# A GRU over 128 steps on one core: r and z as one joint product of seven block products, in one instruction stream

## The chip, the cores and the metric

The kernel runs on one core of a Trainium2 chip. The metric is the device time of one execution in microseconds (us). TensorE (PE in the profile) multiplies matrices and writes to PSUM, VectorE (DVE), ScalarE (ACT) and GpSimd (POOL) work on rows of up to 128 partitions, SyncE (SP) issues DMAs. Each engine takes its instructions in the order in which the program lists them; the order between engines is kept by semaphores.

## The reference

A gated recurrent unit (GRU) with batch 64, 128 steps, 512 inputs and 512 hidden units, all in float32, and a residual sum at the end. Every fourth step but the last the state is passed through one more layer before the next step.

```python
def step(h, inp):
    x_t, prop = inp
    comb = jnp.concatenate([x_t, h], axis=-1)
    z = jax.nn.sigmoid(comb @ Wz + bz)
    r = jax.nn.sigmoid(comb @ Wr + br)
    comb2 = jnp.concatenate([x_t, r * h], axis=-1)
    h_cand = jnp.tanh(comb2 @ Wh + bh)
    h_new = (1.0 - z) * h + z * h_cand
    h_next = jnp.where(prop, jnp.tanh(h_new @ Wp + bp), h_new)
    return (h_next, h_new)
...
do_prop = ((t + 1) % 4 == 0) & (t < T - 1)
out = x + ys
```

## The kernel before

**Layout.** The 64 rows of the batch are two halves of 32 (`h` = 0, 1). TensorE's array is used as four strips of 32 columns: a product of one half is 32 rows high and lies on one strip, and four such products run side by side, each on its own quarter of the partitions. Each float32 product appears as two matmul records (and two weight loads) in the profile.

**Recurrent part.** A gate of one half is `gate(i, h, lT, w)`: four blocks of the hidden size (`K` = 4) times two column groups, 8 products of 256 columns on the half's two strips; the other two strips are left to the other half. A step has three gates for each half, R, Z and the candidate H, and every fourth step P. The products add onto PSUM tiles `rec_0`, `rec_1` and `rec_z` that ScalarE has filled before with the input part of that step (`seed`, from the SBUF tiles `cp`). ScalarE's sigmoid or tanh (`crossed`), VectorE's multiply and transpose (`turn`) lead to the next product of that half.

**Input part.** x times the three input weights doesn't depend on the state. It is worked out for groups of four steps by two nested levels of a seven-product scheme (Strassen's, in Winograd's form): `batch` makes two outer products as 14 units, and a unit has 4 products of 192 columns on all four strips. The units of a batch go to three PSUM banks (scratch tiles) in turn; after certain units ScalarE copies a bank or VectorE adds banks (the `end_` functions) into SBUF tiles `mb`. GpSimd adds these up to `cp` (`outer_...`, `with_bias`) and makes the sums of x that the scheme needs (`sum_...`), and adds the new state to x for the output.

**Order.** `half(h)` is a generator that yields after every product with its cost in columns. A loop at the end runs `half(0)` and `half(1)` side by side and always takes the one that is behind, 700 columns apart, so that the products of the two halves alternate on TensorE, and one half's sigmoid, multiply and transpose pass while the other half's products run. `fill(n, h)` puts n units of the input part in between, by the table `PLACES`, one row for each of eight steps. The last two steps run in `wide_step`, with products of 128 columns.

```python
def half(h):
    for t in range(T):
        ...
        yield from gate(R, h, hT, wh[R])
        ...
        yield from gate(Z, h, hT, wh[Z])
        ...
        yield from fill(places[0], h)
        yield from gate(H_, h, rhT, wh[H_])
        ...
while any(live):
    h = 0 if live[0] and (not live[1] or at[0] <= at[1]) else 1
    cost = next(halves[h], None)
    ...
        at[h] += cost
```

Of the kernel before, what the change touches and what calls it, by code (L numbers as in the profile page):

```python
# [18 lines left out]
def kernel(  # L19
# [14 lines left out]
    nc = tc.nc  # L34
# [6 lines left out]
    J = H // NQ  # L41
    C = 2
    K = D // P
    Q4 = 4
    CHUNK = 4
    FIRST = 2
    LAST = T // Q4 - 1
# [3 lines left out]

    const = ctx.enter_context(tc.tile_pool(name="const", bufs=1))
    xrp = ctx.enter_context(tc.tile_pool(name="xr", bufs=2))
    one = ctx.enter_context(tc.tile_pool(name="one", bufs=1))
    xtp = ctx.enter_context(tc.tile_pool(name="xt", bufs=2))  # L60
    mbp = ctx.enter_context(tc.tile_pool(name="mb", bufs=3))
    two = ctx.enter_context(tc.tile_pool(name="two", bufs=2))
    ps_c = ctx.enter_context(tc.tile_pool(name="ps_c", bufs=1, space=PSUM))
    ctx.enter_context(tc.manual_schedule())

    zeros = one.tile([P, 4 * J], BF16, tag="cq", name="zeros")
# [13 lines left out]
    wh = [const.tile([P, K, H], F32, name=f"wh_{i}") for i in range(3)]  # L80
    wp = const.tile([P, K, H], F32, name="wp")

    tw_all = const.tile([P, 3, S * NQ * 3 * J // 2], F32, name="tw")
# [3 lines left out]
    d5 = const.tile([P, S, NQ, 3, J // 2], F32, name="d5")  # L87
    din = const.tile([P, 3, NQ, 3, J // 4], F32, name="din")
    tt = const.tile([P, 7, 3, NQ, 3, J // 4], F32, name="tt")
    gates_in = (Wr, Wz, Wh)  # L90

    bias_in = tw_all.rearrange("p a b -> p (a b)")[:NQ, : 3 * J].rearrange("q (i j) -> q i j", i=3)
    rest = tw_all.rearrange("p a b -> p (a b)")[:NQ, 3 * J : 6 * J].rearrange("q (i j) -> q i j", i=3)
    middle = const.tile([NQ, 3, J], BF16, name="middle")

    def part(q):
        return slice(q * V, (q + 1) * V)

# [15 lines left out]

    xr = {}

    def new_xr(g):
        xr[g] = xrp.tile([P, Q4, S, J], F32, tag="xr", name=f"xr_{g}")
# [13 lines left out]
    h_rows = tw_all[:, 2, : S * J].rearrange("p (h u) -> p h u", h=S)  # L132
    h_init = two.tile([P, S, J], F32, tag="h", name="h_init")
    bias_x = const.tile([P, C, S, 3, J // 2], F32, name="bias_x")
    bias_p = const.tile([P, S, J], F32, name="bias_p")
# [8 lines left out]
    for i, b in enumerate((br, bh, bz)):  # L144
# [16 lines left out]
    def load_wh(i):  # L161
        load_w(wh[i], gates_in[i][D:])

    xs = {}

    def load_xs(g):
        if g * Q4 < T:
            xs[g] = one.tile([P, Q4, S, J], F32, tag=f"xs{g % 2}", name=f"xs_{g}")
            load_x(xs[g], g * Q4, Q4)

    def later_loads():
        new_xr(1)
        load_x(xr[1], Q4, Q4)
        load_xs(2)
        load_x(xr[0], 0, 2)
        load_w(wp, Wp)
        for q in range(NQ):
            nc.sync.dma_start(
                out=bias_p[part(q)],
                in_=bp.rearrange("(o d c j) -> c o d j", o=1, d=2, c=2)[q % 2].broadcast_to(  # L180
                    [V, S, J]
                ),
            )


    P_ = 3
    rec = [ps_c.tile([P, 2, 2, J], F32, name=f"rec_{n}") for n in ("0", "1", "z")]
    z = rec[2][:, 1]

    def gate_ps(i, h):  # L190
        return rec[2][:, 0] if i == Z else rec[h][:, 0 if i == R else 1]

    scratch = [ps_c.tile([P, 4 * J], F32, name=f"scratch_{n}") for n in "qraxy"]
    q_ps, r_ps, a_ps, *x_two = (
        s[:, : 3 * J].rearrange("p (m h v) -> p m h v", m=2, h=S) for s in scratch
    )
    q_bank, r_bank, a_bank, *x_banks = range(5)
    r_ = scratch[r_bank][:, 3 * J :]

    def quarters(v):  # L200
        return v.rearrange("p n (d c j) -> p c n d j", d=2, c=2)
# [10 lines left out]
    def spread(bank, rows, which):  # L212
        bank = bank.rearrange("p (i d j) -> p i d j", i=len(which), d=2)
        for d in range(2):
            for h in range(S):
                for c in range(2):
                    nc.tensor.matmul(
                        bank[part(2 * h + c), :, d],
                        lhsT=picks[:, 2 * d + c],
                        rhs=thirds[:, rows],  # L220
# [4 lines left out]
        for j, i in enumerate(which):  # L225
            nc.scalar.copy(
                bias_x[:, :, :, i, :].rearrange("p n d u -> p d n u"),
                bank[:, j].rearrange("p d (n u) -> p d n u", n=C),
            )

    bias0 = bias_x[:, 0]
    bias_d = const.tile([P, S, 3, J // 2], F32, name="bias_d")

    def idle(n):
        for i in range(n):
            nc.tensor.matmul(
                rec[i // NQ % 3].rearrange("p a d n -> p (a d n)")[part(i % NQ)],
# [6 lines left out]
    def products(ps, h, left, rhs, start=False):  # L244
        for c in range(2):
            nc.tensor.matmul(  # L246
                ps[part(2 * h + c)],
                lhsT=left,
                rhs=rhs(c),
                start=start,  # L250
                stop=True,
                skip_group_check=True,
            )
# [6 lines left out]
    def product(ps, h, lT, w, k, start=False):  # L260
# [15 lines left out]
    def crossed(dst, h, i, func, ordered=True):  # L276
        for d in range(2):
            o, v = dst[ts(d, 2 * V)], gate_ps(i, h)[ts(h, 2 * V), d, :]
            if ordered:
                o, v = state_order(o), plain_order(v)  # L280
# [937 lines left out]
```

## Time and profile before

| | |
|---|---|
| time, median of 3 runs | 1255.37 us (1254.85 to 1255.91) |
| profiled execution: span from first to last instruction | 1253.6 us |
| busy PE, DVE, ACT, POOL | 1246.9, 806.2, 830.0, 908.8 us |
| granted TensorE clock | full in all 40 slices |

The span of the profiled execution is 1.8 us under the median; what lies around the span is taken as these 1.8 us. In the profile's groups, a row has line, engine, operation, what is written and read, the shape, the count, then busy time in us and the mean of one in ns, then idle time before them. The timeline has start and duration in us. "Busy" of PE is a union over its four strips.

### The profile page before, as it was taken

Reading aid. Unit: us, or ns where it says so; the run is one execution under the profiler, and the core shown is the slowest. Engines: PE = TensorE matmul, PEld = TensorE weight load, DVE = VectorE, ACT = ScalarE, POOL = GpSimd, SP = SyncE. Lnnn points to the kernel's source line nnn. Section 1 sums busy time; section 2 is a strip of 40 time slices with the busy share of each in tenths; the row PEclk is TensorE's granted clock in tenths of the full one; section 3 lists DMA queues with packets and bytes.
Section 4 is the critical chain, followed back from the end, with each engine's and each line's share of the span. In section 5 each row is a group of like instructions: output and inputs, shape, how many; then the busy total and the mean of one; then the engine's idle time right before and its main releaser. Section 6 shows DMA issues by size and latency. Waiting matters only on the chain.

```text
span 1253.6 us, 61573 instructions
## 1 busy us (share of the span) xinstructions
PE 1246.9 (99%) x26384; PEld 1174.0 (94%) x26384; DVE 806.2 (64%) x2177; ACT 830.0 (66%) x2666; POOL 908.8 (72%) x1032
## 2 busy tenths in 40 slices
PE   9999999999999999999999999999999999999998
PEld 5899999999999999999999999999999999999987
DVE  5666666666666666666666666666666666666554
ACT  2566666766666676766666667666666666666664
POOL 4988777777876778767778677786777777777630
PEclk9999999999999999999999999999999999999999
DMA  8311212121111110221201211111111112111011
GB/s 257 83 31 42 53 37 53 36 54 39 35 53 49 41 49 24 53 53 37 54 24 49 53 41 50 36 43 47 53 38 39 49 39 53 39 52 27 12 39 35
DMA packets 112360, 61.14 MB, mean 49 GB/s; under 512 B 12844, under 2 KB 109368, under 8 KB 112088
## 3 DMA queue, kind: packets, MB, share of 16 engines
q1 hardware_dynamic: 111656, 56.90, 16.8%
q8 instruction: 208, 3.41, 1.2%
q14 instruction: 64, 0.52, 0.1%
q0 software_dynamic: 256, 0.14, 0.1%
q10 hardware_dynamic: 176, 0.16, 0.0%
HBM read 40.38 MB, written 16.78 MB: 46 GB/s over the span
## 4 chain that ended last, share of the span: by engine, by line
PE 99%; DMA 1%; SPq 0%; DVE 0%; issue 0%; ACT 0%
PE rec L246 44%; PE rec_z L246 16%; PE scratch_r L246 14%; PE scratch_q L246 11%; PE scratch_a L246 5%; PE scratch_y L246 4%; PE scratch_x L246 4%; DMA wx<-in_L_cond_Wr_dram 1%; PE scratch_a L541 0%; PE scratch_r L541 0%; PE scratch_q L541 0%; PE scratch_y L541 0%; PE scratch_x L541 0%; SPq L127 0%; SPq L141 0%
## 5 line engine op out<-in xcount | busy, mean ns | idle before, releaser
L246 PE MATMUL rec<-wh,rhT 128*32 128x256 f32 x4032 | 370.1, 379 | 0.0
L246 PE MATMUL rec<-wh,hT 128*32 128x256 f32 x3008 | 276.2, 379 | 0.0
L246 PE MATMUL rec_z<-wh,hT 128*32 128x256 f32 x3008 | 276.2, 379 | 0.0
L246 PEld LDWEIGHTS rec<-wh,rhT 128*32 128x32 f32 x4032 | 247.5, 110 | 16.7 <-ACT rec L442 0.3
L281 ACT ACTIVATE scratch_r<-rec 64x128 f32<-64x128 f32 x504 | 126.0, 250 | 129.9 <-PE rec L246 65.4
L442 ACT COPY rec<-cp 64x256 f32<-64x256 f32 x504 | 186.9, 371 | 19.4 <-DVE cp L483 0.2
L246 PEld LDWEIGHTS rec_z<-wh,hT 128*32 128x32 f32 x3008 | 190.5, 110 | 6.2
L246 PEld LDWEIGHTS rec<-wh,hT 128*32 128x32 f32 x3008 | 184.0, 110 | 11.2 <-ACT rec_z L442 0.4
L281 ACT ACTIVATE rec_z<-rec_z 64x128 f32<-64x128 f32 x488 | 122.0, 250 | 91.3 <-PE rec_z L246 79.7
L281 ACT ACTIVATE c<-rec 64x128 f32<-64x128 f32 x504 | 136.7, 271 | 61.5 <-PE rec L246 50.4
L968 POOL TENSOR_TENSOR xr<-xr,h 128x256 f32<-128x256 f32 x125 | 109.3, 874 | 85.8 <-DVE h L1138 71.9
L711 POOL TENSOR_TENSOR cp<-mb,mb 128x768 f32<-128x768 f32 x76 | 139.1, 1830 | 9.4 <-DVE mb L677 5.7
L711 POOL TENSOR_TENSOR mb<-mb,mb 128x768 f32<-128x768 f32 x58 | 106.3, 1832 | 45.8 <-DVE mb L677 45.8
L711 POOL TENSOR_TENSOR cp<-mb 128x768 f32<-128x768 f32 x46 | 84.3, 1832 | 56.8 <-ACT rec_z L442 55.4
L246 PE MATMUL scratch_r<-tw,s 128*32 128x192 f32 x928 | 120.9, 326 | 0.0
L650 ACT COPY cq<-scratch_q 128x384 f32<-128x384 f32 x212 | 102.1, 481 | 19.4 <-PE scratch_q L246 17.9
L667 DVE TENSOR_TENSOR cx<-scratch_r,cx 128x384 f32<-128x384 f32 x106 | 59.0, 557 | 84.5 <-PE scratch_r L246 69.0
L246 PE MATMUL scratch_q<-tt,s 128*32 128x192 f32 x928 | 103.6, 326 | 0.0
L1102 DVE SCALAR_TENSOR_TENSOR keep<-rec_z,h 128x256 f32<-128x256 f32 x91 | 38.6, 424 | 95.6 <-ACT rec_z L281 89.2
L673 DVE TENSOR_TENSOR mb<-scratch_q,cx 128x384 f32<-128x384 f32 x106 | 59.0, 557 | 62.5 <-ACT cq L650 62.5
L1081 DVE TENSOR_TENSOR rh<-scratch_r,h 128x128 f32<-128x128 f32 x188 | 54.8, 292 | 59.2 <-ACT scratch_r L281 59.2
L246 PE MATMUL rec<-wp,hT 128*32 128x256 f32 x992 | 91.4, 379 | 0.0
(250 smaller groups left out, 3899.9 us busy)
## 6 DMA issues: line engine op xcount, KB each, us to landing
out_dram<-xr SPq DMA_DIRECT2D x250, 64.0 KB, 1.8
xr<-in_x_dram SPq DMA_DIRECT2D x248, 64.0 KB, 2.1
xs<-in_x_dram SPq DMA_DIRECT2D x240, 64.0 KB, 2.1
wx<-in_L_cond_Wz_dram SPq DMA_DIRECT2D x2, 512.0 KB
wx<-in_L_cond_Wh_dram SPq DMA_DIRECT2D x2, 512.0 KB, 9.5
wh<-in_L_cond_Wr_dram SPq DMA_DIRECT2D x2, 512.0 KB
wh<-in_L_cond_Wz_dram SPq DMA_DIRECT2D x2, 512.0 KB, 5.5
wh<-in_L_cond_Wh_dram SPq DMA_DIRECT2D x2, 512.0 KB
```

The costliest lines, as they stand in the source:

```text
L246: nc.tensor.matmul(ps[part(2 * h + c)], lhsT=left, rhs=rhs(c), start=start, stop=True, skip_group_check=True,)
L281: nc.scalar.activation(o, v, func)
L442: nc.scalar.copy(gate_ps(i, h)[rows].rearrange("p d (c n) -> p d c n", c=C), G[t][rows, :, :, i, :].rearrange("p c d n -> p d c n"),)
L650: nc.scalar.copy(c[:, :nm], ps[:, :nm])
L667: nc.vector.tensor_add(T2[what][:, :nm], r_ps[:, :nm], T2[what][:, :nm])
L673: nc.vector.tensor_add(blocks(1, 1), runs(q_ps[:, :nm]), runs(T2[what][:, :nm]))
L711: nc.gpsimd.tensor_add(dst, a, b)
L968: nc.gpsimd.tensor_add(o, o, h_new.rearrange("p h (k e) -> p h e k", k=K))
L1081: nc.vector.tensor_mul(rh[:, h, :], r_, h_old[:, h, :])
L1102: nc.vector.scalar_tensor_tensor(out=kept[0], in0=kept[1], scalar=1.0, in1=kept[2], op0=ALU.subtract, op1=ALU.mult,)
```

## The change

Nearly all of the step is written anew. One instruction stream takes the place of the two generators: `step(t, h_old)` lists every instruction of a step in order, and `fill(n)` inserts n units of the input part at six places of a step (eight where P is run), by a new table `PLACES` with four rows.

R and Z are made by one seven-product scheme over both halves of the batch and both halves of the hidden size: seven left factors are kept in `ht` (`S1`, `A11`, `S2`, `A12`, `S3`, `S4`, `A22`, sums of quarters of the transposed state), the right factors are blocks of the joint weights `wrz` and three sums of them, `tr`. `rz(region, slot, right)` is one of the seven, 8 products of 128 columns over all four strips. The results are put together by four VectorE adds in a step (`n1` into `gx`, three into the banks B and C, `row[0]` and `row[1]`), which also add the input part of R and Z; two of them lie between products that add onto the same bank. The roles of the halves alternate: `L` = t % 2, `E` = 1 - t % 2. The candidate and P are `full(...)`, 16 products of 128 columns over all four strips for one half.

The input part keeps its scheme, with other bank use: ScalarE now makes five copies in a batch (`end_1`, `end_5`, `end_2`, `end_3`, `end_4`), VectorE two adds (`end_6`, `end_7`). GpSimd's sums stay in `mb`, and `send` moves them by four DMAs each on SP's queue into `gx`, in the layout of the state. ScalarE copies the candidate's input part from `gx` to PSUM at the end of the step before (`seed_h`). The last steps have no form of their own; the groups 2 to 31 are all made by the scheme.

```diff
+    def four_tiles(region, left, rhs, start=False):
+        for q in range(NQ):
             nc.tensor.matmul(
-                ps[part(2 * h + c)],
+                region[part(q)],
...
-    def gate(i, h, lT, w):
-        for k in range(K):
-            products(gate_ps(i, h), h, lT[:, h, ts(k, V)], lambda c: quarters(w)[:, c, k])
-            yield S * J
...
+        def end_1():
...
+            nc.scalar.copy(a_x, u_x)
+        def end_5():
...
+            nc.scalar.copy(made["e"], e_x)
+        def end_6():
+            nc.vector.tensor_add(e_x, u_x, made["e"])
+        def end_2():
+            nc.scalar.copy(blocks(0, 0), runs(a_x))
+        def end_7():
+            nc.vector.tensor_add(blocks(1, 1), runs(u_x), runs(made["e"]))
+        def end_3():
+            nc.scalar.copy(blocks(0, 1), runs(e_x))
+        def end_4():
+            nc.scalar.copy(blocks(1, 0), runs(u_x))
+        seq = []
+        for ps, j, start, end in (
+            (u_x, 1, True, end_1),
+            (e_x, 5, True, end_5),
+            (u_x, 6, False, end_6),
+            (a_x, 2, False, end_2),
+            (u_x, 7, False, end_7),
+            (e_x, 3, False, end_3),
+            (u_x, 4, False, end_4),
+        ):
...
+    def send(q, n, g, i):
+        new_gx(q)
+        for h in range(S):
+            for d in range(2):
+                nc.sync.dma_start(
+                    out=gx[q][ts(d, 2 * V), :, h, n], in_=M[g, i][ts(h, 2 * V), :, d]
+                )
...
+    def sum_rz():
+        nc.vector.tensor_sub(tr_block(3), wrz_block(0, 1), wrz_block(1, 1))
...
+    def early(v):
+        turn(a21_ps, v[:, : 2 * V])
+        turn(ht[:, A22], v[:, 2 * V :])
+        nc.vector.tensor_add(ht[:, S1], a21_ps, ht[:, A22])
+    def early_copy():
+        nc.scalar.copy(s1_ps, ht[:, S1])
+    def late(v):
+        turn(ht[:, A11 : A12 + 1].rearrange("p n v -> p (n v)"), v)
+        nc.scalar.copy(a12_ps, ht[:, A12])
+        nc.vector.tensor_sub(
+            ht[:, S2 : S3 + 1],
+            s1_a21_ps,
...
-    PLACES = (
-        (1, 7, 6), (1, 7, 0), (6, 8, 0), (6, 8, 0), (1, 8, 5), (1, 7, 0), (6, 8, 0), (6, 6, 0),
-    )
+    PLACES = {
+        0: (2, 2, 2, 1, 1, 3, 0, 0),
+        1: (4, 2, 2, 1, 0, 3, 0, 0),
...
+        3: (4, 2, 2, 1, 0, 2, 2, 1),
+    }
...
+            fill(next(places))
+            rz(e_ps, S1, raw(0, 1), start=True)
+            n1 = G[t][:, :, 1, :2].rearrange("p h g u -> p h (g u)")
+            nc.vector.tensor_add(n1, bcast(e_ps), n1)
+            fill(next(places))
+            rz(u_ps, A11, raw(0, 0), start=True)
+            nc.vector.tensor_add(row[0][:, :J], u_ps, rz_in(t, L, 0))
+            late_2()
+            fill(next(places))
+            rz(u_ps, S2, summed(2))
+            nc.vector.tensor_add(row[0][:, J : 2 * J], u_ps, rz_in(t, L, 1))
+            rz(row[0][:, :J], A12, raw(1, 0))
+            fill(next(places))
+            rz(u_ps, S3, summed(3))
+            nc.vector.tensor_add(
+                row[1][:, : 2 * J].rearrange("p (n j) -> p n j", n=2),
...
+            rz(row[0][:, J : 2 * J], S4, raw(1, 1))
+            gates(0)
+            gates_z(0)
+            fill(next(places))
+            rz(row[1][:, :J], A22, summed(4))
+            gates(1)
+            gates_z(1)
```

Three places show the order. TensorE before, at the start of a step: R of half 0 (`rec_128`) and half 1 (`rec_129`) and then Z, with units of the input part (`scratch`) between them.

```order
L246 MATMUL rec_128<-wh_92,hT_5332 32x256 x2
L246 MATMUL scratch_q<-d_97,o_8_5049 32x192 x2
L246 MATMUL rec_128<-wh_92,hT_5332 32x256 x2
L246 MATMUL scratch_r<-tw,s_8_5052 32x192 x2
L246 MATMUL scratch_r<-d_97,s_8_5052 32x192 x2
L246 MATMUL rec_128<-wh_92,hT_5332 32x256 x2
L246 MATMUL rec_129<-wh_92,hT_5332 32x256 x2
```

TensorE now, from the second candidate of step 20 (`bank_C` from `wc`) into step 21: four units (`x_107`, `x_105`, `x_104`), S1 (`bank_E`), two units, A11 (`bank_A` from `wrz`), two units, S2 (`bank_A` from `tr_89`) and A12 (`bank_B` from `wrz`).

```order
L243 MATMUL bank_C<-wc,rhT_4889 32x128 x16
L503 MATMUL x_107<-wx,s12r_4344 32x192 x4
L503 MATMUL x_105<-tt,xT_4156 32x192 x8
L503 MATMUL x_104<-tw,o_6_4737 32x192 x4
L243 MATMUL bank_E<-wrz,ht 32x128 x8
L503 MATMUL x_104<-wx,o_6_4737 32x192 x4
L503 MATMUL x_107<-tw,s_6_4740 32x192 x4
L243 MATMUL bank_A<-wrz,ht 32x128 x8
L503 MATMUL x_107<-wx,s_6_4740 32x192 x4
L503 MATMUL x_104<-tt,s_6_4740 32x192 x4
L243 MATMUL bank_A<-tr_89,ht 32x128 x8
L243 MATMUL bank_B<-wrz,ht 32x128 x8
```

The halves no longer alternate, and S2 and A12 stand next to each other. In the built program the first matmul of A12 waits for the VectorE add that reads S2 (the one into `row[0][:, J : 2 * J]`, which lies in A12's bank), and the first matmul on `x_107` after S1 waits for ScalarE's copy out of `x_107` (`end_3`).

ScalarE before, over the second half of a step: tanh (`c`), the seeds (`cp`), then two copies of the input part, then the next step's sigmoids.

```order
L281 ACTIVATE c_7984<-rec_128 64x128 x2
L442 COPY rec_128<-cp_7541 64x256
L281 ACTIVATE c_7984<-rec_129 64x128 x2
L442 COPY rec_129<-cp_7541 64x256
L442 COPY rec_z<-cp_7541 128x256
L650 COPY cx_6_8024<-scratch_y 128x384
L650 COPY cq_6_8034<-scratch_q 128x384
L281 ACTIVATE scratch_r<-rec_128 64x128 x2
```

ScalarE now, at the same place of steps 20 and 21: both tanh (`c`), `early_copy` (L724) and `late`'s copy (L728) out of `ht`, two seeds (`gx`), and behind them the input part's `end_3` (from `x_107`), `end_4`, `end_1` and `end_5`.

```order
L902 ACTIVATE c_4890<-bank_B 128x128
L902 ACTIVATE c_4890<-bank_C 128x128
L724 COPY bank_B<-ht 128x64
L728 COPY bank_C<-ht 128x64
L745 COPY bank_B<-gx_4409 128x128
L745 COPY bank_C<-gx_4409 128x128
L532 COPY mb_1_4900<-x_107 128x2x6x32
L535 COPY mb_1_4900<-x_105 128x2x6x32
L516 COPY x_106<-x_104 128x384
L520 COPY e_6_5121<-x_107 128x384
```

The copies of the input part now stand behind four copies that belong to the state, and the second of these waits for the state's last transpose.

VectorE now, at that place: `keep`, the transpose of x (`xT`), `end_7` (L529), then the first half's multiply, subtract, two short transposes and add (`early`), the second half's multiply, subtract and transpose (`late`), and `late`'s subtract.

```order
L879 SCALAR_TENSOR_TENSOR keep_4891<-bank_A,hprop_4795 128x256
L262 STREAM_TRANSPOSE xT_5000<-xs_3885 128x2x4x32
L529 TENSOR_TENSOR mb_1_4900<-x_105,e_1_4919 128x2x6x32
L903 TENSOR_TENSOR bank_A<-c_4890,bank_A 128x128
L904 TENSOR_TENSOR h_5015<-bank_A,keep_4891 128x128
L239 STREAM_TRANSPOSE bank_B<-h_5015 128x64
L239 STREAM_TRANSPOSE ht<-h_5015 128x64
L721 TENSOR_TENSOR ht<-bank_B,ht 128x64
L903 TENSOR_TENSOR bank_A<-c_4890,bank_A 128x128
L904 TENSOR_TENSOR h_5015<-bank_A,keep_4891 128x128
L239 STREAM_TRANSPOSE ht<-h_5015 128x128
L729 TENSOR_TENSOR ht<-bank_B,ht 128x128
```

What the input part needs of VectorE (here `end_7`) stands in one list with the state's chain, and in other steps behind it.

More of the change, by code (lines that the diff above doesn't have):

```diff
@@ L130, in load_wx, with load_xs @@
         )
[L132 to L135, printed above, removed]
+    def load_xs(g):
+        if g < GROUPS:
+            xs[g] = one.tile([P, Q4, S, J], F32, tag=f"xs{g % 2}", name=f"xs_{g}")
+            load_x(xs[g], g * Q4, Q4)
     new_xr(0)
@@ L536 @@
[L536 to L553 removed]
+    gx, G = {}, {}
@@ L1182 @@
+    task("s12_2", lambda: [sum_s12(2), did.add(("s12", 2))], "pair1", 28, after=tuple(("join", 2, i) for i in range(4)))
+    task(("free73", 0), lambda: None, "pair2", 14)
+    for d in range(DUOS):
+        sums(d)
+    fill(4)
+    h = h_init
+    for t in range(T):
+        if t == 1:
+            load_xs(3)
+        h = step(t, h)
 _INS = [
```

1225 lines of the change are left out of this document (525 added, 700 removed), and 5 rows, old and new, of tables (HEAD, PLACES).

## The prediction

> **What bounds the kernel now.** I read the page first, then stretches of time, the groups by shape, one tile's rows, and the timeline of the last steps, which have products of 128 columns.
>
> ```profile
> PE 1246.9 (99%) x26384; PEld 1174.0 (94%) x26384; DVE 806.2 (64%) x2177; ACT 830.0 (66%) x2666; POOL 908.8 (72%) x1032
> ...
> PE 99%; DMA 1%; SPq 0%; DVE 0%; issue 0%; ACT 0%
> ```
> ```profile
> core 0: us, PE busy (x) PEld busy (x) DVE busy (x) ACT busy (x) POOL busy (x), PEclk, DMA share, GB/s
> 71.80:1224.10 1152.30, 1152.30 (x24282) 1099.02 (x24277) 748.72 (x2013) 787.13 (x2529) 855.39 (x968) 1.00 0.16 43
> 1224.10:1253.60 29.50, 25.42 (x758) 23.01 (x750) 14.06 (x48) 12.20 (x43) 2.61 (x3) 1.00 0.14 35
> ```
> ```profile
> L246 PE MATMUL rec<-wh,hpT x992: 376/379/403, 71.8 to 1225.0; 128*32 128x256 f32 x199
> ```
>
> TensorE is the bound: it is never idle from 71.8 us, where step 4 begins (its R is the first product with `hpT`), to the start of step 124, whose R ends with the last such record at 1225.0 and so starts near 1224.1. These 120 steps take 1152.3 us, 76.8 for eight. A gain must come from fewer columns; a loss comes from anything that makes TensorE wait.
>
> **Prices.** Rows of the timeline (start, duration):
>
> ```profile
> 602.31 0.55 DVE L676 TENSOR_TENSOR mb<-scratch_r,cq 128x384 f32<-128x384 f32 x1
> 602.78 0.55 DVE L677 TENSOR_TENSOR mb<-scratch_y,cq 128x384 f32<-128x384 f32 x1
> ```
> ```profile
> 1240.95 0.28 PE L541 MATMUL scratch_r<-wh,rhT 128*32 128x128 f32 x2
> ...
> 1241.83 0.28 PE L541 MATMUL scratch_q<-wh,hT 128*32 128x128 f32 x2
> ...
> 1242.70 0.28 PE L541 MATMUL scratch_r<-wh,rhT 128*32 128x128 f32 x2
> ```
> ```profile
> 1243.33 0.31 DVE L284 STREAM_TRANSPOSE hT<-h 128x128 f32<-128x128 f32 x1
> ...
> 1243.69 0.30 PE L541 MATMUL scratch_a<-wh,hT 128*32 128x128 f32 x2
> ```
> ```profile
> 1248.44 1.08 PE L541 MATMUL scratch_y<-wh,rhT 128*32 128x128 f32 x28
> ...
> 1249.57 0.28 ACT L1045 ACTIVATE c<-scratch_y 128x128 f32<-128x128 f32 x1 [0.59 <-PE scratch_y L541]
> 1249.88 0.29 DVE L1046 TENSOR_TENSOR z<-c,z 128x128 f32<-128x128 f32 x1
> 1250.20 0.29 DVE L1052 TENSOR_TENSOR xr<-z,xr 128x128 f32<-128x128 f32 x1
> ```
>
> A product of 16 matmuls of 128 columns (32 records) starts every 0.87 us: eight waves of four records, 0.109 each. So `full` costs 0.87, `rz` (half as many) 0.436, and a unit (8 records of 192 columns, so two waves 1.5 times as wide) 2 × 1.5 × 0.109 = 0.327; I take 0.325. As a test, eight steps of before are 26 gate products of 1.744 and 98 units: 77.2, 0.5% over the 76.8.
>
> A result travels so: the last record of a product ends at 1249.52, ScalarE starts at 1249.57; a record lasts 0.27 and starts one wave before the product's end, so a reader starts 0.27 + 0.05 - 0.11 = 0.21 after TensorE could go on. ScalarE to VectorE and VectorE to itself take 0.03. TensorE starts 0.05 after the transpose that it waits for, and its next wave comes 0.02 late. VectorE operations that don't need each other overlap by 0.08 (602.31 + 0.55 against 602.78).
>
> ```profile
> L284 DVE STREAM_TRANSPOSE rhT<-rh 128x128 f32<-128x128 f32 x256 | 79.8, 312 | 8.8
> L297 DVE STREAM_TRANSPOSE xT<-xs 128x256 f32<-128x256 f32 x120 | 74.7, 642 | 2.2 <-issue 0.4
> L1136 DVE TENSOR_TENSOR rec_z<-c,rec_z 128x128 f32<-128x128 f32 x244 | 71.8, 294 | 17.9 <-ACT c L281 14.3
> ...
> L676 DVE TENSOR_TENSOR mb<-scratch_r,cq 128x384 f32<-128x384 f32 x106 | 58.0, 547 | 0.2 <-PE scratch_r L246 0.2
> ...
> L1102 DVE SCALAR_TENSOR_TENSOR keep<-rec_z,h 128x256 f32<-128x256 f32 x91 | 38.6, 424 | 95.6 <-ACT rec_z L281 89.2 <-PE rec L246 6.3
> ...
> L354 DVE TENSOR_TENSOR d<-wx 128x768 f32<-128x768 f32 x2 | 1.8, 951 | 0.0
> ```
> ```profile
> L281 ACT ACTIVATE c<-rec 64x128 f32<-64x128 f32 x504 | 136.7, 271 | 61.5 <-PE rec L246 50.4
> L281 ACT ACTIVATE scratch_r<-rec 64x128 f32<-64x128 f32 x504 | 126.0, 250 | 129.9 <-PE rec L246 65.4 <-DVE mb L676 50.5 <-DVE rhT L284 0.6
> ...
> L650 ACT COPY cq<-scratch_q 128x384 f32<-128x384 f32 x212 | 102.1, 481 | 19.4 <-PE scratch_q L246 17.9
> L442 ACT COPY rec_z<-cp 128x256 f32<-128x256 f32 x126 | 47.5, 377 | 41.0 <-DVE h L1138 36.3 <-DVE cp L483 4.1 <-POOL cp L711 0.6
> ```
>
> Two shapes have no row. A ScalarE copy of 128 columns I take as 0.27 and one of 64 as 0.20, on the line through 0.377 (256) and 0.481 (384). A transpose of 64 lies between 0.16 and 0.31; I take 0.20, since its cost falls nearly with its columns.
>
> **The change part by part.**
>
> *Fewer columns.* R and Z of a step cost 7 × 0.436 = 3.05 for 3.49. TensorE's work for eight steps is 8 × 3.05 + 16 × 0.872 (candidate) + 4 × 0.872 (P) + 98 × 0.325 = 73.7: 3.1 less than 76.8.
>
> A page speaks against products half as wide: the Trainium skill, "TensorE: Matmul & The Clock Gate", "Back-to-back issue gap", gives about 81 ns per matmul of 128 columns when each has its own weight load. By that figure the 24,900 records of 128 columns of the new kernel alone would take about 2.0 ms (an estimate from that page). The rows above differ, 0.87 us for 32, or 27 ns, with four strips side by side; the measurement decides.
>
> *A12 behind S2.* Nothing stands between them, and A12 waits for the VectorE add that reads S2: 0.21 + 0.29 + 0.05 + 0.02 = 0.57 in each of 127 steps. Before, the other half's products lay there.
>
> *A22 behind the add of 256 columns.* 0.21 + 0.42 + 0.07 = 0.70 after S3; S4 hides 0.44. Where no unit stands there (six steps of eight) 0.26 is left. The other adds between products are covered by one or two units, and so are the chains to the candidates (sigmoid, multiply, transpose: 1.25 from A22 against 1.85) and, with four units and S1 ahead, to A11.
>
> *Units behind the end of a step.* This is the largest term. 49 units for four steps and 14 for a batch: the pattern repeats after eight steps, 4 to 11, 12 to 19 and so on. Take step 21 (5 in the first pattern). Zero is the end of step 20's second candidate. VectorE has `keep` 0.42, the transpose of x 0.64 and `end_7` 0.55 ahead of the first half's multiply, which starts at 0.07. Then: multiply and subtract 0.66, two transposes 0.36, add 0.14 before the next overlaps it, multiply and subtract 0.66, transpose 0.35: 2.24. There `late`'s subtract and ScalarE's copy start; the seeds wait for the subtract: 2.56 and 2.86; `end_3` runs from 3.16 to 3.64. The unit that writes its bank again can start at 3.73. TensorE is there after four units, S1 and one unit, at 2.17. It waits 1.56, and the whole stream with it. The same sum for the others, with what each unit waits for:
>
> step 4: `end_1` 0.18. 5: `end_3` 1.56. 6: `end_7` 1.66. 7: `end_7` 0.65, first P 0.13. 8: none. 9: `end_6` 0.91. 10: `end_6` 1.06. 11: `end_1` 1.56, first P 0.54. Sum 8.3.
>
> *Eight steps:* 73.7 + 8 × 0.57 + 6 × 0.26 + 8.3 + some 25 restarts of 0.02 and S1's 0.05 = 88.8, against 76.8. Bounds: transposes of 0.16 give 88.4; no overlap on VectorE gives 92.9; if ScalarE and VectorE reach the end of a step 0.5 us earlier, six waits shrink by 3.0 to 85.8.
>
> *The sums by DMA.* Copies to `cp` go, four DMAs for each come.
>
> ```profile
> L711 POOL TENSOR_TENSOR cp<-mb,mb 128x768 f32<-128x768 f32 x76 | 139.1, 1830 | 9.4 <-DVE mb L677 5.7
> ```
> ```profile
> L102 SPq DMA_DIRECT2D xr<-in_x_dram x256: 311/432/1773, 19.8 to 1201.5; - x128
> ```
> ```profile
> xr<-in_x_dram SPq DMA_DIRECT2D x248, 64.0 KB, 2.1
> ```
>
> The tightest is the second block of an even group, in the step ahead of its use: two adds 3.7, four issues 1.7, landing 2.1: 7.5 us, with about 9 until ScalarE needs it. Nothing, if the landing stays under 3.6. If not, ScalarE stands at the seed, and behind it the copies and the sigmoids.
>
> *Head.* Three sums and one difference of the joint weights (1024 columns, 1.23 each on the slope of the 0.951 row) and four transposes of x stand in step 0 ahead of VectorE's multiply, the differences of the input weights and four transposes in step 1. TensorE has some 5 us of cover for 17; waits as above fall in steps 1 to 3. I add 9 us (0 to 20): step 4 starts at 81.
>
> *Tail.* All units are used up by step 124. Steps without cover wait for S1 1.0, A11 0.4, S2 and A12 0.6 each, A22 0.3, the candidate 0.5, beside 4.8 of work: 8.3, the first 7.3. After the last product 4.1 as before (1249.5 to 1253.6): 36.3 for 29.5.
>
> *Sum:* 81 + 15 × 88.8 + 36.3 = 1449 as the span, and 1.8 around it: 1451 us.
>
> **The rivals.**
>
> *Copies in time.* Only A12 and A22 wait fully, and units a tenth of it (1.5). Eight steps 81.4, in all 81 + 1221 + 36 + 2 = 1340. For it: ScalarE is busy 66% now, and has idle time. Against it: its copies stand in one list behind the state's chain. Chance 0.12.
>
> *Late sums.* A landing of 4 to 6 us makes one seed in eight steps wait 1 to 3: 1466 to 1496. For it: SP issues 16 more DMAs for four steps. Against: the DMA engines are 16% busy. Chance 0.14.
>
> *Narrow products.* The weight load ends up beside the stream instead of under it.
>
> ```profile
> L246 PEld LDWEIGHTS rec<-wh,rhT 128*32 128x32 f32 x4032 | 247.5, 110 | 16.7 <-ACT rec L442 0.3 <-ACT scratch_r L281 0.2
> ```
>
> One load takes 110 ns, 6,200 on each strip: up to 0.68 ms more, 2.1 ms. This is the page's rule as a mechanism of this kernel; the 0.87 above speaks against it. Chance 0.02.
>
> *Fed all the same (faster).* If TensorE doesn't stand at A12 and at the units, because results return within what is queued, only the columns count: 76 + 15 × 73.7 + 33 + 2 = 1216. It decides where the waits of eight steps sum to less than 3.1, a quarter of my sum; A12's alone, with nothing queued between, is 4.6. Chance 0.04, with 0.01 of it near the tie.
>
> **How the numbers follow.** My forecast has 0.68, and the time is its own, 1451. The range 1370 to 1510 holds nearly all of it, with the bounds 85.8 and 92.9 (1406 to 1513), the head's bounds and the late sums; the other 0.18 are outside. Measurement can tell 0.2% from no change: faster 0.03, same 0.01, slower 0.96.
>
> **What would show it.** Right: PE idle before the product that writes bank B after S2, about 0.57 for each, released by the VectorE add into bank B; idle before units, released by the ScalarE copies and by `end_6` and `end_7`; 88 to 89 us between every second P; a last stretch of about 36. Wrong: PE idle released by DMA or GpSimd, a wave of more than 0.11, or eight steps near 81 or 74.

## The result: 1504.3 us, 1.198 times the time before

The changed kernel takes 1504.29 us (median of 4 runs, 1501.6 to 1508.97), the kernel before 1255.64 beside it: a ratio of 1.198, 95% interval 1.196 to 1.201. The forecast was 1451 with a range of 1370 to 1510, so the time lies 6 us inside its upper bound. The profiled execution took 1501.6 with a span of 1499.8.

The page of the changed kernel: busy times, the chain that ended last, and the granted clock by slice.

```profile
PE 1284.1 (86%) x37368; PEld 1096.2 (73%) x37368; DVE 892.5 (60%) x2864; ACT 566.2 (38%) x1959; POOL 924.5 (62%) x1051
...
PEclk9999999999999999999999999999999999999999
...
PE 55%; DVE 25%; issue 8%; ACT 4%; DMA 3%; POOL 2%; DVEq 1%; SPq 1%; ACTq 0%; POOLq 0%
```

TensorE, 99% busy before, is 86% busy, and the chain that was 99% TensorE now runs for a quarter through VectorE. A row of the next view has a stretch and its length, busy times in the order PE, PEld, DVE, ACT, POOL, and the granted clock third from the end. 88.7 is the start of S1 of step 4, 1460.2 that of step 124.

```profile
40.30:88.70 48.40, 42.31 (x1112) 35.18 (x1116) 27.04 (x77) 15.95 (x52) 33.66 (x38) 0.97 0.23 62
88.70:1460.20 1371.50, 1184.48 (x34792) 1016.14 (x34780) 816.79 (x2666) 532.92 (x1843) 861.75 (x982) 1.00 0.29 72
1460.20:1499.80 39.60, 24.30 (x712) 18.07 (x704) 21.27 (x75) 9.44 (x41) 7.92 (x6) 0.97 0.21 49
```

The 120 steps take 1371.5 us, 91.4 for every eight where before took 76.8. What TensorE waited for is in its table of waits (who waited and for whom, idle time in us, how often, the longest):

```profile
PE bank_B L243 <- DVE bank_B L848: 61.9, 126, 0.6
PE x L503 <- DVE mb L529: 36.2, 30, 1.8
PE x L503 <- DVE x L523: 33.2, 31, 3.6
PE x L503 <- ACT x L516: 20.8, 15, 1.4
PE x L503 <- ACT mb L532: 17.6, 15, 1.3
PE bank_C L243 <- DVE bank_C L852: 13.1, 64, 0.2
```

These are the three kinds of wait that the prediction named: A12 (first row), units (L503, four rows), A22 (last). No wait of the steps is put down to a DMA. How two waits for A12 look in the timeline (start, duration, and in brackets idle time and who ended it):

```profile
297.25 0.64 PE L243 MATMUL bank_A<-tr,ht 128*32 128x128 f32 x16
297.97 0.30 DVE L848 TENSOR_TENSOR bank_B<-bank_A,gx 128x128 f32<-128x128 f32 x1 [0.64 <-PE bank_A L243]
298.32 0.64 PE L243 MATMUL bank_B<-wrz,ht 128*32 128x128 f32 x16 [0.42 <-DVE bank_B L848]
```
```profile
307.83 0.64 PE L243 MATMUL bank_A<-tr,ht 128*32 128x128 f32 x16
308.55 0.30 DVE L848 TENSOR_TENSOR bank_B<-bank_A,gx 128x128 f32<-128x128 f32 x1 [0.64 <-PE bank_A L243]
308.96 0.41 PEld L243 LDWEIGHTS bank_B<-wrz,ht 128*32 128x32 f32 x16 [0.75 <-ACT mb L535]
308.99 0.64 PE L243 MATMUL bank_B<-wrz,ht 128*32 128x128 f32 x16 [0.51 <-DVE bank_B L848]
```

In the first, S2 starts at 297.25 and TensorE could go on 0.44 later; A12 starts at 298.32, so the wait is 1.07 - 0.44 = 0.63. The table shows 0.42 for it: it counts idle time from the end of the last record, which here lies 0.2 behind the moment at which TensorE could have gone on, so each wait costs 0.2 more than its row. In the second, the wait is 1.16 - 0.44 = 0.72.

Counted so from start to start between 88.7 and 1460.2, TensorE's waits in eight steps come to 5.6 us at A12 (0.63 to 0.81 a step, 0.70 on average), 8.3 at units, 2.3 at A22 and 0.9 at the first product of P. The table agrees: for A12 (61.9 + 126 × 0.2) / 15.9 = 5.5 over the whole run, and for the units, without the one wait of 3.6 ahead of step 4, (104.2 + 90 × 0.2) / 15 = 8.1.

The products themselves have the forecast's price: of the 4,612 waves of 128 columns in these steps the median is 0.109, and 4,401 take 0.112 or less; nearly all others are the first wave of a product, at 0.13.

### The profile page after: what moved, and what is told of

It reads as the page before. It is cut to its first block, busy times and chain, and to the rows that moved or that the text cites. A ratio compares the mean times of both kernels' runs of the same rounds, so it can differ in the third digit from the quotient of the medians.

```text
span 1499.8 us, 85372 instructions
## 1 busy us (share of the span) xinstructions
PE 1284.1 (86%) x37368; PEld 1096.2 (73%) x37368; DVE 892.5 (60%) x2864; ACT 566.2 (38%) x1959; POOL 924.5 (62%) x1051
## 4 chain that ended last, share of the span: by engine, by line
PE 55%; DVE 25%; issue 8%; ACT 4%; DMA 3%; POOL 2%; DVEq 1%; SPq 1%; ACTq 0%; POOLq 0%
PE x L503 22%; PE bank_B L243 13%; PE bank_A L243 10%; PE bank_C L243 8%; DVE h L904 3%; DVE bank_C L852 3%; DVE bank_A L903 3%; DVE bank_B L848 3%; DVE ht L239 2%; DVE mb L529 2%; DMA gx<-mb 2%; DVE x L523 2%; DVE bank_B L239 1%; PE bank_E L243 1%; DVE ht L729 1%
## 5 line engine op out<-in xcount | busy, mean ns | idle before, releaser
L561 POOL TENSOR_TENSOR mb<-mb,mb 128x768 f32<-128x768 f32 x167 | 304.1, 1825 | 152.1 <-ACT mb L535 138.2
L243 PE MATMUL bank_B<-wrz,ht 128*32 128x128 f32 x4128 | 165.0, 275 | 63.1 <-DVE bank_B L848 61.9
L243 PEld LDWEIGHTS bank_B<-wrz,ht 128*32 128x32 f32 x4128 | 111.9, 109 | 95.7 <-DVE bank_B L848 42.7
L243 PE MATMUL bank_A<-tr,ht 128*32 128x128 f32 x4064 | 162.2, 275 | 1.9 <-DVE bank_B L844 1.9
L503 PE MATMUL x<-tt,s 128*32 128x192 f32 x1920 | 120.6, 328 | 50.4 <-DVE x L523 29.6
L243 PE MATMUL bank_B<-wc,rhT 128*32 128x128 f32 x4096 | 137.2, 273 | 1.4 <-ACT bank_E L766 1.0
L243 PE MATMUL bank_C<-wc,rhT 128*32 128x128 f32 x4096 | 137.2, 273 | 0.0
L243 PEld LDWEIGHTS bank_A<-tr,ht 128*32 128x32 f32 x4064 | 115.6, 110 | 29.0 <-DVE bank_B L844 22.2
L243 PEld LDWEIGHTS bank_B<-wc,rhT 128*32 128x32 f32 x4096 | 120.2, 110 | 7.3 <-ACT bank_E L766 1.7
L243 PEld LDWEIGHTS bank_C<-wc,rhT 128*32 128x32 f32 x4096 | 116.2, 110 | 0.2
L503 PEld LDWEIGHTS x<-tt,s 128*32 128x32 f32 x1920 | 61.3, 110 | 66.8 <-ACT x L516 24.8
L523 DVE TENSOR_TENSOR x<-x,e 128x384 f32<-128x384 f32 x108 | 60.0, 556 | 62.1 <-PE x L503 47.1
```

The costliest lines, as they stand in the source:

```text
L243: nc.tensor.matmul(region[part(q)], lhsT=left, rhs=rhs(q), start=start, stop=True, skip_group_check=True,)
L503: nc.tensor.matmul(v[part(2 * h + c)], lhsT=left[:, ts(h, V)], rhs=right[:, c::2], start=start and m == 0 and n == 0, stop=True, skip_grou ...
L523: nc.vector.tensor_add(e_x, u_x, made["e"])
L561: nc.gpsimd.tensor_add(flat(M[g, i]), flat(M[g, i]), flat(M[g2, j]))
```

## The experiments

**e1: A12 ahead of the add that reads S2.**

```diff
             rz(u_ps, S2, summed(2))
-            nc.vector.tensor_add(row[0][:, J : 2 * J], u_ps, rz_in(t, L, 1))
             rz(row[0][:, :J], A12, raw(1, 0))
+            nc.vector.tensor_add(row[0][:, J : 2 * J], u_ps, rz_in(t, L, 1))
```

> Edit: A12 stands ahead of the VectorE add that reads S2, so A12 no longer waits for it; the add now waits for A12, and S3 for the add. Theory (the order in which readers and writers of a bank are listed makes TensorE wait, and the waits add up): the 126 waits of A12 (61.9 us idle in the trace of the change, 5.2 us per eight steps) go, and S3 takes over a smaller one, 0.25 + 0.30 + 0.05 behind A12 less the one unit of 0.33, about 0.28 a step or 2.2 per eight: 88 us for eight steps, 1504 - 48 = about 1455 us. Rival (the follow-ups of the units, tied to the end of a step, set the pace): what A12 no longer waits the units wait longer, no change, 1495 to 1504. Rival (chain of the state alone): A12's 0.44 leaves the chain from the first to the last product of a step, the same 1455; this run does not tell that from the theory.

Measured: 1455.28 us, ratio to before 1.159 (1.157 to 1.161); eight steps 88.2 (here and below the median of the groups of eight steps, from every second P to the next). The theory's number, to the microsecond. TensorE's waits in this run:

```profile
PE x L503 <- DVE mb L529: 36.2, 30, 1.7
PE x L503 <- ACT x L516: 19.4, 15, 1.4
PE x L503 <- ACT mb L532: 18.4, 15, 1.3
PE x L503 <- DVE x L523: 17.3, 16, 3.6
PE x L503 <- POOL o L366: 16.0, 15, 1.1
```

The row of A12 is gone, and the rows of the units are nearly what they were: they did not take over the time. S3 waits instead, mostly too shortly for the table to list it. The second row below is S3; the unit ahead of it costs 0.33, so S3 starts 0.27 late, where the theory has 0.28:

```profile
302.31 0.51 PE L503 MATMUL x<-wx,xT 128*32 128x192 f32 x8
302.91 0.65 PE L243 MATMUL bank_A<-tr,ht 128*32 128x128 f32 x16
```

From step 4 to 123, S3's waits come to 2.3 for eight steps, and at A12 only restarts of 0.02 are left. As the expectation says, this run alone does not tell the theory from a chain of the state alone. One wait of the units changed hands. Half of those for L523 are now put down to GpSimd's sum of x (L366), which ends last there.

**e2: the first units of a step ahead of the copies that end the step before.** `PLACES_0` is the first number of the next step's row.

```diff
+        fill(PLACES_0(t + 1))
         early_copy()
         late(h_new[:, E])
         seeds()
...
-            fill(next(places))
+            next(places)
             rz(e_ps, S1, raw(0, 1), start=True)
```

> Edit: the units that open a step are listed, with their ScalarE copies and VectorE adds, ahead of the copies and the subtract that end the step before; TensorE's own order is the same. Theory (units wait because their copies stand behind the state's in one list): the waits of units (8.8 us per eight steps in the trace of the change, the first P's among them) fall to 3 to 4, eight steps near 86, 1504 - 86 = about 1418 us. Rival (ScalarE and VectorE are simply late, whatever the order): the copies of 0.48 and adds of 0.55 now delay the state by as much as they gain, 1490 to 1520; if they delay it in every step by 0.5, 127 x 0.5 = 64 slower, up to 1570.

Measured: 1416.82 us, ratio 1.128 (1.126 to 1.129); eight steps 86.0. TensorE's waits:

```profile
PE bank_B L243 <- DVE bank_B L851: 65.6, 127, 0.6
PE bank_C L243 <- DVE bank_C L855: 19.3, 95, 0.2
PE x L503 <- DVE mb L529: 15.0, 15, 1.0
PE x L503 <- DVE x L523: 7.2, 16, 1.8
```

The waits for ScalarE's copies (L516, L532) are gone and those for VectorE a third: 22 us in all where 108 stood. The copies were not late because ScalarE had too much to do, but because they stood behind the state in its list.

**e3: narrow units.** A unit's products have 32 columns for 192.

```diff
-                        v[part(2 * h + c)],
+                        v[part(2 * h + c)][(slice(None), 0, 0) if g >= 4 else ...],
                         lhsT=left[:, ts(h, V)],
-                        rhs=right[:, c::2],
+                        rhs=right[:, c, 0] if g >= 4 else right[:, c::2],
```

> Edit: from the fourth group on, each product of a unit has 32 columns for 192; every copy, add, wait and DMA stays. The sums of the input part are incomplete. If TensorE's columns set the time, eight steps lose 98 x 0.27 = 26.5 us, about 1504 - 400 = 1100. Theory (waits behind results): what the units no longer cover becomes waiting. A step without any unit took 8.80 us at the end of the changed kernel's trace, and a step with P takes some 2.5 more: 6 x 8.8 + 2 x 11.3 = 75 for eight steps is the least, and the waits of units stay partly: 78 to 84, so 1300 to 1390 us.

Measured: 1503.45 us in its one run, no change at all. Neither number came. The stretches show two instances of one kind of step (steps 30 and 38, both third in a pattern of eight that begins with step 4), with the granted clock third from the end:

```profile
386.51:397.22 10.71, 9.18 (x280) 7.95 (x281) 5.24 (x18) 3.26 (x11) 3.59 (x2) 0.68 0.12 34
480.48:489.28 8.80, 6.78 (x281) 5.86 (x281) 5.27 (x18) 3.14 (x10) 3.60 (x2) 1.00 0.14 37
```

The same 280 records take 10.71 us at a clock of 0.68 and 8.80 at 1.00. In a slow stretch a product of 16 records starts 0.84 after the one before, where 0.44 is the rule:

```profile
709.36 1.09 PE L243 MATMUL bank_A<-tr,ht 128*32 128x128 f32 x16
710.20 1.11 PE L243 MATMUL bank_B<-wrz,ht 128*32 128x128 f32 x16
```

So the columns that were taken out came back as waits and as a slower clock: groups of eight steps took 88.5 us at a mean clock of 0.94 and 94 at 0.82. At the full clock the theory's floor stands: the shortest instance of each of the eight kinds of step, all at a clock of 0.99 or 1.00, was 9.35, 12.09, 8.80, 11.68, 8.90, 9.94, 10.16 and 12.48, together 83.4, against 91.4, though TensorE had 26.5 less to do.

**e4: the same edit on the kernel before.**

> The same edit on the kernel before: the units' products have 32 columns for 192 from the fourth group on, all else stays; the sums of the input part are incomplete. If columns alone bound it, eight steps fall from 76.8 by 26.5 to 50, about 1255 - 410 = 850 us; GpSimd alone is busy for 909 and so the floor is above that. Theory: two streams hide each other's chains; the chain of one half sets a floor lower than the 76.8, and lower than that of the changed kernel: 1000 to 1190 us. Rival (the kernel before stands at its chain's floor as well, and the columns were only just as long): 1240 to 1255.

Measured: 1171.04 us, one run. The stretch of the 120 steps, and TensorE's largest wait:

```profile
70.00:1134.00 1064.00, 961.80 (x24199) 780.02 (x24194) 741.49 (x2013) 782.81 (x2526) 853.72 (x967) 1.00 0.18 46
```
```profile
PE rec L246 <- DVE hT L284: 78.8, 97, 1.2
```

Eight steps took 70.6 (the median; the first group, whose units are in part still wide, 78), where columns alone would be 50. So the kernel before has a floor as well, and its largest wait is for the transposes of its own state, but the floor lies below its 76.8 of columns. The changed kernel's 83.4 at full clock lies above its 73.7. The change lowered the columns by 3 and raised by 13 what the kernel, in this order of its instructions, doesn't go under. Whether two streams or plain products give the lower floor, these two runs do not tell.

**e5: the edits of e1 and e2 together.**

> Edit: the edits of the first two runs together (A12 ahead of the add; the first units of a step, with their copies and adds, ahead of the copies that end the step before). Theory (separate waits that add up): the two gains add, 49 + 87 = 136, 1504 - 136 = about 1368 us, and eight steps near 82.5. Rival (one chain is behind both, so that what one edit frees the other waits for): less than the sum, 1390 to 1417 us.

Measured: 1367.65 us, ratio 1.088 (1.086 to 1.090). The two gains, 49 and 87.5, add to within a microsecond, so the rival, one chain behind both, is out.

**e6: one stream with plain products of r and z.** Each half's gate is `full`, 16 products, as in `first_step`; ScalarE seeds r, z and the candidate in one copy. The table `PLACES` is another one, the roles of the halves no longer alternate, and the sums of weights in the first step go.

```diff
-            rz(e_ps, S1, raw(0, 1), start=True)
-            ...
-            rz(row[1][:, :J], A22, summed(4))
+            plain_product(0, R)
+            gates(0)
+            fill(next(places))
+            plain_product(1, R)
+            gates(1)
+            fill(next(places))
+            plain_product(0, Z)
+            gates_z(0)
+            fill(next(places))
+            plain_product(1, Z)
+            gates_z(1)
...
-            early(h_new[:, L])
+            turn(hT[:, ts(L, J)], h_new[:, L])
```

> Edit: the joint seven-product scheme for r and z undone alone; one instruction stream, the sums by DMA and the input part stay. r and z are 8 block products in full width for each half, seeded by ScalarE; a unit or two between them. TensorE's columns are those of the kernel before, about 77 us for eight steps. Theory (the seven products are made one after another from sums and put together by adds, and each such add is a wait): the stream of plain products has next to no waits, since R of one half covers the other half's transpose and Z covers R's sigmoid, multiply and transpose: 78 to 79.5 for eight steps, 1275 to 1315 us in all. Rival (one stream in place of two is what fails to hide the chains): eight steps near 88 or more, 1450 us or more.

Measured: 1306.96 us, ratio 1.041 (1.039 to 1.043); eight steps 79.6.

```profile
PE 1274.6 (98%) x39400; PEld 1148.7 (88%) x39400; DVE 644.1 (49%) x1844; ACT 592.7 (45%) x1705; POOL 925.2 (71%) x1051
```

With 8 × 0.436 = 3.5 us more columns for eight steps this form is 197 us faster than the change, and TensorE is 98% busy: one stream as such does not fail to hide the chains. The 4% that are left to the kernel before hold the one stream, the sums by DMA (ScalarE's seeds wait for them 17 times here, 19.2 us) and a table that was not searched for; these were not told apart. The joint product, in one stream and in this order, costs the rest.

**e7: one wait less in the state's chain.**

```diff
-                out=keep, in0=z_ps, scalar=1.0, in1=h_old, op0=ALU.subtract, op1=ALU.mult
+                out=h_new, in0=z_ps, scalar=1.0, in1=h_old, op0=ALU.subtract, op1=ALU.mult
...
-            nc.vector.tensor_sub(h_new[:, h], z_h, keep[:, h])
+            nc.vector.tensor_sub(h_new[:, h], z_h, h_new[:, h])
```

> Edit: VectorE writes keep into the tile of the new state, so that keep, off the chain, waits for GpSimd to be done with that tile, and the first half's subtract waits for its multiply alone. Theory (a second wait in front of an operation costs time even where it was met long ago: in the trace of the change the first half's subtract, with two waits, starts 0.11 us after its multiply, and the second half's, with one, 0.04): the gap falls to 0.04, the state comes 0.06 us earlier in 127 steps, where the chain is waited for: 1496 to 1500 us, and in any case the rows of the trace show 0.04. Rival (the 0.11 belongs to the first half's operands or to what runs beside it): the gap stays 0.11 and the time 1502 to 1509.

Measured: 1492.99 us (1490.03 to 1496.47), ratio 1.189 (1.186 to 1.191), against 1.198 (1.196 to 1.201). VectorE's timeline of the changed kernel, multiply and subtract of both halves in one step:

```profile
600.54 0.30 DVE L903 TENSOR_TENSOR bank_A<-c,bank_A 128x128 f32<-128x128 f32 x1 [0.33 <-ACT c L902]
600.95 0.29 DVE L904 TENSOR_TENSOR h<-bank_A,keep 128x128 f32<-128x128 f32 x1
...
601.89 0.28 DVE L903 TENSOR_TENSOR bank_A<-c,bank_A 128x128 f32<-128x128 f32 x1
602.21 0.29 DVE L904 TENSOR_TENSOR h<-bank_A,keep 128x128 f32<-128x128 f32 x1
```

And of e7:

```profile
597.91 0.29 DVE L905 TENSOR_TENSOR bank_A<-c,bank_A 128x128 f32<-128x128 f32 x1
598.24 0.29 DVE L906 TENSOR_TENSOR h<-bank_A,h 128x128 f32<-128x128 f32 x1
```

The first half's subtract started 0.11 after its multiply (600.95 - 600.84) and now starts 0.04 after it (598.24 - 598.20); the median over 127 steps falls from 104 to 34 ns. The row of line 904 in the changed kernel shows what stood between:

```profile
L904 DVEq EVENT_SEMAPHORE  x125: 21/21/21, 70.6 to 1485.8; - x125
```

An instruction of its own on VectorE's queue carries one of the two waits; e7 has none for its line 906. 0.07 a step is 9 us; the spans of the two profiled executions differ by 8.6, the medians by 11, and the intervals don't meet. The time lies 3 us under the theory's range. The operands are not the cause: the second half's subtract has the same ones in the changed kernel and started 0.04 after its multiply.

**e8: all edits, and units put where the rows show waits.** `PLACES` has eight rows, and its first number is the units ahead of the end of the step before:

```diff
-        0: (2, 2, 2, 1, 1, 3, 0, 0),
-        1: (4, 2, 2, 1, 0, 3, 0, 0),
+        0: (2, 0, 2, 2, 2, 2, 1, 0, 0),
+        1: (3, 1, 1, 2, 2, 0, 3, 0, 0),
...
+        7: (5, 0, 1, 1, 2, 1, 2, 3, 0),
```

> Edit: the edits of the other runs (A12 ahead of the add, first units ahead of the end of a step, keep in the state's tile) and a table of eight rows that puts units where the rows of the trace show waits: two between A12 and S3, one or two ahead of A22, none where they wait themselves. Theory (waits only, no floor above the columns): eight steps 79 to 79.5 for 91.4, 1504 - 15.5 x 12 = about 1318 us, 1300 to 1330. Rival (a floor of the state's chain: bare steps of 8.80 and P steps of some 11.3 would be 75 for eight steps, and 83 was the sum of the shortest steps with narrow units): not under 82, 1360 us or more. Neither gets under the 1255 of before: for that eight steps would have to take under 74.9, since the first steps and the last take 90 and 40 us.

Measured: 1341.49 us, ratio 1.069 (1.066 to 1.071); eight steps 80.9. Better than e5 by 26, and 23 short of the theory; neither number came, for the rival's 82 is out as well. The rows of the sums' DMAs in this run:

```profile
  DVE gx L866: 12.8, 12
  ACT bank_C L759: 12.0, 12
...
DMA to landing us min/median/max: 2.2/2.6/4.3
```

VectorE's first add and ScalarE's seed now wait for the DMAs into `gx`, once in most groups of eight steps, and `end_7` with the unit behind it. The late sums, a rival of the prediction, appear where the steps are short, here and in e6.

**e9: the loads of x moved away from those DMAs.**

```diff
-                    load_xs(g + 2)
+                    later_x.append((steps_done + 2, g + 2))
```

> Edit: e8 with the eight DMAs that load x for a later group listed one to two steps later on SyncE's queue, so that they no longer run beside the four sends of the last sum of an even group. In the trace of e8 the fourth of these sends took 4.2 us to land (2.2 is the rule), and VectorE's first add waited 12 times for it, 12.8 us, ScalarE's seeds another 12.0. Theory (the late sums, priced as a rival in the prediction, come true once the steps are fast): these waits fall below 4 us each, the unit that stood behind them no longer waits, eight steps 79.5 to 80, 1341 - 15 to 25 = about 1320 us. Rival (GpSimd's sum is late, not the transfer): the sends are issued as late as before and the time stays 1335 to 1345.

Measured: 1341.61 us (1337.74 to 1342.74), the rival's number.

```profile
  DVE gx L869: 9.9, 10
  ACT bank_C L760: 9.9, 10
...
DMA to landing us min/median/max: 2.2/2.4/4.4
```

The loads of x were not the cause. For one such wait in e8, this is what GpSimd does ahead of it:

```profile
446.14 3.74 POOL L575 TENSOR_TENSOR mb<-mb,mb 128x768 f32<-128x768 f32 x2 [3.01 <-ACT mb L549]
```

GpSimd stood for 3.01 until ScalarE had made the batch's last copy (`end_4`). Two adds of 1.87 follow, then four DMAs, issued from 449.9 to 452.0. The last of them landed at 456.2, 4.2 us after its issue, and then VectorE goes on:

```profile
456.31 0.42 DVE L866 TENSOR_TENSOR gx<-bank_E,gx 128x256 f32<-128x256 f32 x1 [2.26 <-DMA gx<-mb]
```

So the rival's number came, but its cause is at most a part of it. With a landing of 2.2, as the other three have within 0.1, the DMA would have been there at 454.2, when VectorE had waited 0.2 of its 2.26: the rest is the slow landing. Worked out so for all twelve waits of e8 (every DMA of the four landing after 2.2), 4.1 of the 12.8 us are left. What makes a landing slow is open, and neither an earlier end of the batch nor another way of sending was tried.

**e10: units of half the width** (96 columns, the edit of e3 with `(slice(None), 0)` and `right[:, c]`).

> Edit: the changed kernel with units of 96 columns for 192 from the fourth group on (the sums of the input part are incomplete), between the change itself and e3 with 32. Columns fall by 98 x 0.163 = 16 us for eight steps. In e3 the granted clock was 0.85 to 0.91 for most of the run, products took twice as long in stretches, and the time did not change. Theory (the clock falls when TensorE is idle for too large a share, and the state's chain sets the rest): if the clock stays full here, eight steps are 85 to 86 and the time 1410 to 1425 us; if it falls as in e3, 1440 to 1505, with a granted clock under 0.95 in the profile. Rival (a floor of some 91 us whatever the columns, the clock only by the way): 1495 to 1505 with a full clock.

Measured: 1440.21 us at a mean clock of 0.985, between the two cases of the theory. Of the groups of eight steps between the first and the last, the four at a clock of 1.00 took 85.8 to 86.6, near its 85 to 86, those at 0.98 86.6 to 87.6, and the two at 0.96 88.7 and 90.1. The floor of 91 whatever the columns is out.

## Why the prediction was right, and what it had too small

- **The mechanism holds.** TensorE has fewer columns and stands still for them: behind S2 (e1), behind copies that stand behind the state (e2), each a wait of its own (e5). Without the joint product's chain of sums, adds and banks, one stream has next to no waits (e6).
- **A12, 0.57 a step forecast, 0.70 measured; 5.6 for eight steps against 4.6.** The failed step is the handing over, at both ends. The first is the 0.21 from the moment at which TensorE could go on to the reader's start. It was worked out as 0.27 + 0.05 - 0.11, as if the four strips ran in step; the last of them starts up to 0.05 behind the first, and VectorE's add starts 0.25 to 0.28 after that moment (297.97 - 297.69 in the rows above). The second is the 0.05 from VectorE to TensorE. It holds in 60 of the 127 steps. In the other 67, A12 has a second wait, for a copy of ScalarE that was done long before, and starts 0.15 after the add's end: 308.99 - 308.85, where the first row pair has 298.32 - 298.27.
- **A22: six steps of eight, 0.26 each forecast.** Six of eight steps have 0.30 to 0.43, 2.3 for eight steps against 1.6, and for the same two reasons: A22 too has a second wait in half of these steps, and then starts 0.15 after the add's end for 0.05.
- **Units: 7.6, and 0.7 for the first P, forecast; 8.3 and 0.9 measured.** The largest term was right in its cause and 0.9 too small.
- **Second waits were not priced at all.** Beside those of TensorE, 0.07 in each step's chain on VectorE; e7 gives 9 to 11 us for one of them.
- **What is left** of 91.4 - 73.7 = 17.7 after 5.6, 2.3, 8.3 and 0.9 is 0.6, for which 0.7 was forecast.
- **Eight steps: 91.4 against 88.8.** Fifteen times 2.6 are 39 of the 53 us by which the forecast was low; head and tail are 10, and the median lies 3 above the profiled execution.
- **The range held in part by luck.** The prediction's upper bound rests on 92.9 for eight steps, from a case with no overlap on VectorE. The overlap is there in the changed kernel (a transpose starts at 601.34 and lasts 0.26, and the next one starts at 601.51); what lengthened the steps were terms that the prediction had too small or had left out, all to the same side.
- **Head: forecast 81, measured 88.** Step 4 starts two units, 0.65, ahead of its S1 at 88.7, so at 88.05. Waits were guessed at 9 us as a whole; one alone, behind VectorE's weight sums and transposes, is 3.6 of idle:

```profile
58.92 0.86 PE L503 MATMUL x<-tt,s12r 128*32 128x192 f32 x16 [3.58 <-DVE x L523]
```

- **Tail: 36.3 forecast, 39.6 measured.** From step 124 on no step has units. Its S1 starts at 1460.2, and the next are 9.1, 8.8 and 8.8 apart, where the sum has 8.3 (it puts the wait for S1 at 1.0); from the last to the end it is 12.9, where the sum has 7.3 and 4.1:

```profile
1469.36 0.64 PE L243 MATMUL bank_E<-wrz,ht 128*32 128x128 f32 x16 [1.24 <-DVE ht L721]
...
1478.16 0.64 PE L243 MATMUL bank_E<-wrz,ht 128*32 128x128 f32 x16 [0.98 <-DVE ht L721]
...
1486.94 0.64 PE L243 MATMUL bank_E<-wrz,ht 128*32 128x128 f32 x16 [0.97 <-DVE ht L721]
```

- **The rivals.** Copies in time (1340): no; even with the order of e2 the kernel takes 1417, and the units still wait for 22 us. Late sums did not occur in the changed kernel: single DMAs of the sums landed after up to 4.2 us, but in the tables of waits GpSimd alone stands for them, twice, 0.6 us in all. The chain that ended last runs over such a DMA once in eight steps, 2% of the span, since it lands just as ScalarE comes to the seed. They did occur in e6 and e8. Narrow products: the median wave of 128 columns kept its 0.109. Fed all the same: no.
- **No version with complete sums beats the kernel before.** With a head of 90 and a tail of 40, eight steps would have to take 74.9; the best of the joint product took 80.9, and plain products in one stream 79.6.

## What to carry to other kernels

Before a product is split so that TensorE has fewer columns, count what has to come back before the next part can start, and compare that time with the columns saved: here 3.1 us were saved and 17.7 of waiting came in. In one stream that is run in order, the follow-ups of filler work (here ScalarE's copies and VectorE's adds behind the units) should be listed ahead of work that waits for the state; moving them was worth 87 us here without one instruction less. Count the waits in front of each operation of the chain as well: a second one cost 0.07 to 0.09 each time, even when it was long met.

## What the runs showed of the hardware

- A second wait in front of an operation took time of its own, also where what it waited for was long done: on VectorE 0.07 us (104 against 34 ns in 125 of 127 steps; e7 took it away), and on TensorE 0.09 us (A12 starts 146 ns after the add's end in 67 steps, 54 in the other 60; no run took it away).
- With narrow units (e3) the granted clock fell without a long idle time. Two stretches of 50 us:

```profile
550.00:600.00 50.00, 36.00 (x1362) 31.71 (x1360) 30.37 (x100) 19.91 (x70) 31.44 (x35) 0.97 0.31 77
...
650.00:700.00 50.00, 38.34 (x1232) 33.85 (x1236) 28.32 (x93) 17.98 (x63) 28.76 (x34) 0.81 0.27 66
```

  TensorE is 72 to 77% busy here, and after the first 60 us its longest idle time is 2.53 us. In the changed kernel, 86% busy, the clock is 1.00. The width of the products alone isn't it: in e4, with the same narrow products and TensorE 90% busy, the mean clock is 0.999. The Trainium skill, "TensorE: Matmul & The Clock Gate", "HAM oscillation — how this bites in real kernels", gives idle gaps of more than about 3.4 us as its abstract rule for a lower clock; here none is that long, and the measurement decides: in e3, shorter gaps that come often went with a lower clock. Which share of idle time it takes was not measured; e10, with TensorE 79% busy, stands at 0.985. e3 is one run.
- The DMAs of the sums (96 KB each, four in turn, some 0.65 us apart) landed after 2.2 us at best, 2.2 in the median of the changed kernel and 2.6 in e8, and after up to 4.2 to 4.4 us in the changed kernel, e8 and e9. It is not always the same one of the four, and what makes one slow is open.
